# Layer 1 of a four-layer graph network in 64x64 tiles of the TensorE array, with one block of targets open at a time

## The chip, the cores and the metric

The kernel runs on one core of one Trainium2 chip. The metric is the device time of one execution in microseconds; a kernel's time is the median over its runs. A profile is one execution taken by the hardware profiler. In it PE is TensorE's matmuls and PEld its weight loads, DVE is VectorE, ACT is ScalarE, POOL is GpSimd, and SP is SyncE, which here issues the loads.

## What is computed

Four graph layers run one after the other over 4096 nodes with 64 features each. All use the same dense 4096 x 4096 matrix `adj` of float32 (64 MiB), and each has a layer norm and a relu in front and a residual behind. The change lies in layer 1, and touches the end of layer 0:

```python
# layer 0
h = relu(layernorm(x));  x = x + relu((adj @ h) @ W0.T + b0)
# layer 1
h = relu(layernorm(x))
h = lorentz_linear(h, W, b, scale)            # 64 -> 64, rows normed
q = lorentz_linear(h, Wq, bq, scale_q)
k = lorentz_linear(h, Wk, bk, scale_k)
att = 2.0 + 2.0 * (qm @ k.T)                  # qm: q with its first column negated
att = adj * sigmoid(att / att_scale + att_bias)
support = att @ h
x = x + support / sqrt(clip(abs(inner(support))))
```

Layer 2 needs all pairwise distances on a Poincare ball and the row sums of `adj` (the degrees); layer 3 needs, for each row, the rank of its nonzeros. Neither is edited.

## The kernel before

**Tiling.** `adj` comes transposed, sources on partitions, targets along the free dimension. A block `ib` is 512 targets (`W`), and there are 8 of them. A group `g` is 256 sources: a tile of 128 partitions x 2 x 512 (`G` = 2), one load of 512 KB, and there are 16 per block. Layer 1 works in pairs of groups, so 8 pairs per block and 64 in all. In this document A stands for the attention matmuls of one pair and S for its sums; the fifth A is that of the fifth pair.

**One pair of layer 1.** `l1_atts` puts q against k into PSUM (tile `mm`). The contraction is 64 long, so the two row halves of the array hold two chunks of 128 sources at once: tiles of 64 rows x 128 columns, 4 matmuls in the program for a pair, which the profile shows as 8 instructions, since one f32 matmul of 512 columns is two. `l1_sigmoids` reads PSUM on ScalarE and writes `sig`. `l1_weights` multiplies `sig` by `adj` on VectorE ("weighing"). `l1_sums`, through `pair_sum`, multiplies by h (`HL`), with a contraction of 128 and 64 output rows: the two column halves of the array hold two chunks at once, tiles of 128 rows x 64 columns. The lower half of the partitions of the accumulator `acc` holds the sum over the even chunks, the upper half that over the odd ones. `after1` evicts `acc` on ScalarE and adds the two halves with a matmul by `twice` (two identities on top of each other).

**Buffers.** PSUM has two `mm` tiles of two banks each, so one pair is in flight there. Up to six `sig` tiles are in use (`SIG`), and a sigmoid waits for the sum six groups back. There are two accumulator banks, taken by `ib % 2`, for layer 0 as for layer 1, so a new block's sums can begin while the old block is evicted. `adj` has ten load buffers in these two layers; a buffer is free when its last reader has run.

**Order.** Loads are issued on SP in the order of the list `order`: the last `EARLY` groups of layer 0 alternate with the first groups of layer 1. The list `l1` sets the order of layer 1's work: blocks 0 and 1 first take their groups 0 to 13 (`BEHIND` = 14), then both take groups 14 and 15, and from block 2 on every block is taken whole. Groups 14 and 15, a block's eighth pair, are sources 3584 to 4095, so they need h, q and k of block 7, whose row work is the last to come out of layer 0. That row work is `after0` and `before1`: eviction, projection by W0T, layer norm, transposition (h), projection by W1T, norms, transposition (HL), projection by WqkT, norms, transpositions (qq, k). Each step is handed from TensorE to ScalarE, VectorE or POOL, which takes square roots and powers. While it runs, `after1` and `before2` of other blocks may run as well, two at a time. Degrees are summed on VectorE (`dg`), some groups in layer 0 and some in layer 1.

A planner (`in_turn`) issues the whole program once, step by step, always the step that can start first by its own estimates; each engine then runs its instructions in exactly that order. So the order is fixed before the run, and an instruction that waits holds everything behind it on its engine.

Of the kernel before, what the change touches and what calls it, by code (L numbers as in the profile page):

```python
# [19 lines left out]
D = 64  # L20
# [3 lines left out]
NB = N // W  # L24
CB = W // P
G = 2
NG = NC // G
LEFT = (3, 7, 11, 15)
FRONT = (4,5,6,7,)
WAIT = 0.6  # L30
EARLY = 12
BEHIND = NG - CB // G
LATE = BEHIND - CB // G
HG = NG // 2
# [15 lines left out]
ON_V, ON_S = "DVE", "ACT"  # L50
# [94 lines left out]
def kernel(ctx: ExitStack, tc: tile.TileContext, a: dict, out: bass.AP):  # L145
# [4 lines left out]
    pace = Pace()  # L150
    PE, DVE, ACT, POOL = (
        InOrder(tc, e, pace, name)
        for e, name in (
            (nc.tensor, "PE"), (nc.vector, "DVE"), (nc.scalar, "ACT"), (nc.gpsimd, "POOL"),
        )
    )
# [144 lines left out]
    def cs(ib):  # L301
        return slice(ib * CB, (ib + 1) * CB)

    def ws(ib):
        return slice(ib * W, (ib + 1) * W)
# [4 lines left out]
    def rt(name, shape, dtype=F32):  # L310
        return rows.tile(shape, dtype, tag=f"{name}_{slot['now']}", name=name, bufs=1)
# [7 lines left out]
    def power(out, v, p):  # L319

        POOL.tensor_tensor(out, v, halves[p][:, 0 : v.shape[1], :], ALU.pow)
# [28 lines left out]
    def bank():  # L350
        k = spare.pop(0)
        t = (ps_two if k else ps_tr).tile([P, W], F32, tag=f"tr{k}", name="tr")
        in_use.append((t, k))
        return t
# [241 lines left out]

    def after1(ib, acc, st):
        e = rows.tile([P, W], F32, tag="e", name="e")
        ACT.copy(e, acc)
        st["acc_free"][ib % 2] = pace.latest  # L600
        yield ON_V, lambda: st["dg_done"].get((1, ib)) if (1, ib) in st["dg"] else 0.0
        dg = st["dg"].get((1, ib))
        if dg is not None:
            DVE.tensor_add(dg[:, 0, :], dg[:, 0, :], dg[:, 1, :])
        yield TURN
        ps = bank()
        v, n = ps[:, 0 : CB * D].rearrange("p (c k) -> p c k", k=D), CB * D
        for c in range(CB):
            b = slice(c * P, (c + 1) * P)
            PE.matmul(v[:, c, :], e[:, b], twice, start=True, stop=True)  # L610
            if dg is not None:
                PE.matmul(ps[:, n + c : n + c + 1], dg[:, 0, b], ones_f, start=True, stop=True)
        if dg is not None:
            st["dg_free"][ib % 2] = pace.latest
        yield ON_S
        s = rt("h", [P, CB, D])
        ACT.copy(s, v)
        sq = rt("r_sq", [P, CB, D])
        ACT.activation(sq, v, AF.Square)
        if dg is not None:  # L620
            new = rt("r_c", [P, CB, 1])
            ACT.copy(new, ps[:, n : n + CB].unsqueeze(2))
        yield ON_V
        if dg is not None:
            DVE.tensor_add(deg[:, cs(ib), :], deg[:, cs(ib), :], new)
        n = rt("r_n", [P, CB, 1])
        DVE.tensor_reduce(n, sq[:, :, 1:D], AX.X, ALU.add)
        DVE.tensor_sub(n, n, sq[:, :, 0:1])
        m = rt("r_m", [P, CB, 1])
        DVE.tensor_scalar(m, n, -1.0, None, ALU.mult)  # L630
        DVE.tensor_max(n, n, m)
        DVE.tensor_scalar(n, n, 1e-08, None, ALU.max)
        power(n, n, -0.5)
        yield ON_V
        DVE.tensor_mul(s, s, n.to_broadcast([P, CB, D]))
        DVE.tensor_add(x[:, cs(ib), :], x[:, cs(ib), :], s)
        yield ON_V
# [69 lines left out]
    def follow(gen, on=ON_V, evicts=False):  # L707

        tail.append(
            {"gen": gen, "on": on, "at": pace.latest, "slot": None, "evicts": evicts, "need": None}  # L710
        )
# [24 lines left out]
    def latest(*times):  # L736
        return None if None in times else max(times)
# [36 lines left out]
    def keep_warm(wait):  # L774
# [14 lines left out]
    st = {  # L789
        "h0": HA[:, :, 0:D],  # L790
        "dg": {}, "dg_done": {}, "acc_free": [0.0, 0.0], "dg_free": [0.0, 0.0],
    }
# [3 lines left out]
    def with_mark(layer, ib, *gens):  # L796
        for gen in gens:
            yield from gen
        rows_at[layer, ib] = pace.latest
# [30 lines left out]
    def take(k, d):  # L830

        return st["acc_free"][k] if d["first"] else 0.0
# [6 lines left out]
    def pair_tile(d):  # L839
        pair_tiles.append(d)  # L840
        turn = mm["count"] = mm["count"] + 1
        if mm["third"] is not None:
            d["ps"] = (ps_mm if turn % 3 else mm["third"]).tile([P, G, W], F32, tag="mm", name="mm")
        else:
            d["ps"] = ps_mm.tile([P, G, W], F32, tag="mm", name="mm")

    def pair_tiles_free():

        n = 2 if mm["third"] is None else 3
        a, b = (d.get("read") for d in pair_tiles[-n:][:2])  # L850
        return latest(a, None if b is None else b - 0.8)

    def acc_tile(k):
        return (ps_two if k else ps_acc).tile([P, W], F32, tag=f"acc{k}", name="acc")
# [17 lines left out]
    def group(layer, ib, g):  # L872
        degree = (g in (LEFT if ib else FRONT) and ib < NB - 1) == (layer == 1)
        return {"layer": layer, "ib": ib, "g": g, "degree": degree, "left": 1 + degree, "at": 0.0}
# [1 line left out]


    l0 = [group(0, ib, g) for ib in range(NB) for g in range(NG)]
    l1 = [group(1, ib, g) for ib in range(2) for g in range(BEHIND)]
    l1 += [group(1, ib, g) for ib in range(2) for g in range(BEHIND, NG)]  # L880
    l1 += [group(1, ib, g) for ib in range(2, NB) for g in range(NG)]
    order = l0[: len(l0) - EARLY] + [d for pair in zip(l0[len(l0) - EARLY :], l1) for d in pair]
    order += l1[EARLY:]
    done = {}
# [6 lines left out]
    accs = {}  # L891


    def pair_sum(d, by, t):
        k = d["layer"], d["ib"]
        if d["first"]:
            accs[k] = acc_tile(d["ib"] % 2)
            st["acc_free"][d["ib"] % 2] = None
        for c in range(G):
            PE.matmul(  # L900
                accs[k][c * D : (c + 1) * D, :], by[:, d["g"] * G + c, :], t[:, c, :],
                start=d["first"], stop=d["last"], skip_group_check=True,
            )
        return accs[k]

    def degree_sums(layer, work):
# [25 lines left out]
    def l0_sums():  # L932
        for d in l0:
            yield "PE", lambda: latest(
                arrival(d), rows_at.get((0, d["g"] * G // CB)), take(d["ib"] % 2, d),
                None if d["last"] and loads else 0.0,
            )
            acc = pair_sum(d, st["h0"], d["adj"])
            used(d)
            if d["last"]:  # L940
                ib = d["ib"]
                follow(with_mark(1, ib, after0(ib, acc, st), before1(ib, st)), ON_S, evicts=True)
# [17 lines left out]
    def l1_atts():  # L960
        for pair in pairs:
            yield "PE", lambda: latest(
                *(rows_at.get((1, d["g"] * G // CB)) for d in pair),
                rows_at.get((1, pair[0]["ib"])), pair_tiles_free(),
            )
            for d in pair:
                pair_tile(d)
                for c in range(G):
                    half = slice(c * D, (c + 1) * D)
                    PE.matmul(  # L970
                        d["ps"][:, c, :], st["kT"][half, d["g"], :],
                        st["qT"][half, ws(d["ib"])], start=True, stop=True,
                    )
                d["dist"] = pace.latest

    def l1_sigmoids():
# [15 lines left out]
    def l1_sums():  # L992
        for pair in pairs:
            yield "PE", lambda: latest(
                *(d.get("weighed") for d in pair), take(pair[0]["ib"] % 2, pair[0])
            )
            for d in pair:
                acc = pair_sum(d, st["HL"], d["att"])
                d["summed"] = pace.latest
            if d["last"]:  # L1000
                ib = d["ib"]
                follow(with_mark(2, ib, after1(ib, acc, st), before2(ib, st)), ON_S, evicts=True)
# [483 lines left out]
    def l3_sum():  # L1486
# [15 lines left out]
        if d["last"]:  # L1502
            follow(after3(ib, acc, st), ON_V, evicts=True)

    last = work[L3_AT:]
    order23 = work[:L3_AT] + [d for pair in zip(last, l3) for d in pair] + l3[len(last) :]
    in_turn([
        feed(order, "early"), feed(order23, "second"), second_tables(), second_part(), third_part(), third_tile(), l2_loads2(),
        l0_sums(), l1_sums(), l1_weights(), l1_sigmoids(), l1_atts(),
        in_steps(  # L1510
            (l2_dists(), -1, once), (l2_signs(), 0, once), (l2_sums2(), 2, if_two(1)),
# [58 lines left out]
```

## Time and profile before

Three runs took 1110.67 to 1120.76 us, median 1119.69. The profiled execution took 1116.49 us, of which its span is 1114.8.

| view | what | value |
|---|---|---|
| times | profiled execution / its span | 1116.49 / 1114.8 us |
| timeline | last layer 0 sum starts / last layer 1 sum ends | 207.2 / 482.8 us |
| groups | `mm<-qT,kT`, 512 instructions | 129.8 us busy, 624 ns each |
| groups | `acc<-sig,HL`, 512 instructions | 124.2 us busy, 605 ns each |
| groups | `sig<-mm` on ScalarE, 128 | 148.6 us busy, 1201 ns each |
| groups | `sig<-sig,adj` on VectorE, 128 | 152.6 us busy, 1221 ns each |
| groups | `e<-acc` copy on ScalarE, 128 x 512 | 586 ns each |
| groups | `e<-acc,others` add on VectorE, 65 x 512 | 682 ns each (layer 2) |
| DMA | `adj` loads | 512 x 512 KB, 5.5 us from issue to landing |

How to read it: a matmul instruction's length holds its way through the array, so two that follow each other overlap, and the time which a group takes is read from the start of one group to the start of the next. Successive operations on ScalarE and VectorE overlap by about 0.1 us for the same reason: sigmoids start 1.10 us apart and weighings 1.14. A shape such as `64*128` is the array's rows x columns that the instruction uses. The bracket at the end of a timeline row is the engine's idle time before it and what ended it.

### The profile page before, as it was taken

What the parts mean: (1) busy time and instruction counts of PE and PEld (TensorE: products, weight loads), DVE (VectorE), ACT (ScalarE), POOL (GpSimd) and SP (SyncE); (2) the same over time, 40 slices, a digit from 0 to 9 for tenths busy, and PEclk for the clock granted to TensorE, in tenths of its full rate; (3) what the DMA queues carried; (4) which work ended last, traced back from release to release, by engine and by line L of the source; (5) the groups of instructions that cost most, each with busy time, mean ns of one, the idle gap of its engine ahead of it and who ended that gap; (6) DMA issues with size and microseconds to landing.
All of it is one profiled execution on the core that took longest, in us unless ns stands there. A gap on an engine that the chain in (4) does not pass through costs nothing.

```text
span 1114.8 us, 15471 instructions
## 1 busy us (share of the span) xinstructions
PE 1053.7 (95%) x5300; PEld 471.2 (42%) x5300; DVE 917.6 (82%) x1496; ACT 795.5 (71%) x1279; POOL 259.9 (23%) x151
## 2 busy tenths in 40 slices
PE   6789999999999999999999999999999987999998
PEld 3234443334233333344454454544444443444444
DVE  7678989878998888758998999989989999766651
ACT  1045545686776777689988888879798776677776
POOL 3022222011111100043334334344443430000000
PEclk9899999999999999999999999999999999999999
DMA  8899999966677677544443444443435539999950
GB/s 305 314 365 409 407 383 363 325 229 225 218 235 244 235 255 248 177 164 163 159 170 141 181 172 144 176 170 138 183 120 217 177 129 353 378 409 409 411 238 10
DMA packets 77191, 271.76 MB, mean 244 GB/s; under 512 B 10040, under 2 KB 11064, under 8 KB 77112
## 3 DMA queue, kind: packets, MB, share of 16 engines
q1 hardware_dynamic: 75456, 270.57, 65.6%
q8 instruction: 42, 0.69, 0.2%
q10 hardware_dynamic: 1656, 0.20, 0.1%
q14 instruction: 37, 0.30, 0.1%
HBM read 269.68 MB, written 1.05 MB: 243 GB/s over the span
## 4 chain that ended last, share of the span: by engine, by line
PE 52%; DVE 19%; issue 8%; DMA 7%; ACT 7%; POOL 6%; SPq 0%; ACTq 0%; POOLq 0%; DVEq 0%
PE acc L137 26%; PE mm L137 16%; PE tr L137 11%; DMA adj<-in_adjT_dram 7%; POOL v L137 5%; DVE t L137 3%; DVE w L137 3%; DVE sig L137 3%; DVE dg L137 3%; ACT t L137 1%; ACT v L137 1%; ACT sig L137 1%; ACT lo_sq L137 1%; POOL lo_s L137 1%; DVE r_n L137 1%
## 5 line engine op out<-in xcount | busy, mean ns | idle before, releaser
L137 PE MATMUL acc<-w,HA 128*65 128x256 f32 (+1 forms) x736 | 247.9, 472 | 10.8 <-DVE w L137 10.7
L137 POOL TENSOR_SCALAR v<-v 128x1024 f32<-128x1024 f32 (+1 forms) x72 | 171.1, 2376 | 269.1 <-ACT v L137 269.1
L137 ACT ACTIVATE sig<-mm,att_b,att_a 128x1024 f32<-128x1024 f32 x128 | 148.6, 1201 | 50.8 <-PE mm L137 50.3
L137 DVE TENSOR_TENSOR sig<-sig,adj 128x1024 f32<-128x1024 f32 x128 | 152.6, 1221 | 29.9 <-ACT sig L137 28.0
L137 ACT ACTIVATE wt<-mm,down 128x1024 fp32r<-128x1024 f32 x128 | 136.1, 1111 | 44.3 <-PE mm L137 41.9
L137 DVE TENSOR_TENSOR dg<-dg,adj 128x1024 f32<-128x1024 f32 x113 | 137.7, 1221 | 7.6 <-DMA adj<-in_adjT_dram 6.0
L137 PE MATMUL acc<-adj,HA 128*64 128x512 f32 x512 | 125.7, 618 | 14.4 <-DMA adj<-in_adjT_dram 14.4
L137 PEld LDWEIGHTS acc<-w,HA 128*65 128x65 f32 x736 | 94.3, 138 | 95.1 <-issue 50.8
L137 PE MATMUL mm<-qT,kT 64*128 64x512 f32 x512 | 129.8, 624 | 2.8 <-ACT sig L137 2.0
L137 PE MATMUL acc<-sig,HL 128*64 128x512 f32 x512 | 124.2, 605 | 1.7 <-DVE sig L137 1.5
L137 ACT ACTIVATE v<-v,minus 128x1024 f32<-128x1024 f32 x72 | 79.1, 1098 | 30.1 <-POOL v L137 28.7
L137 DVE SCALAR_TENSOR_TENSOR t<-mm,t 128x1024 f32<-128x1024 f32 x72 | 83.5, 1160 | 19.7 <-PE mm L137 11.0
L137 DVE SCALAR_TENSOR_TENSOR t<-t,v 128x1024 f32<-128x1024 f32 x72 | 83.3, 1157 | 3.9 <-ACT t L137 3.4
L137 DVE TENSOR_TENSOR w<-t,adj 128x1024 f32<-128x1024 f32 x72 | 84.4, 1173 | 1.4
L137 DVE TENSOR_TENSOR w<-tr,adj 128x512 f32<-128x512 f32 x120 | 77.5, 683 | 8.5 <-PE tr L137 8.4
L137 ACT ACTIVATE t<-t 128x1024 f32<-128x1024 f32 x72 | 72.2, 1003 | 14.3 <-DVE t L137 14.2
L137 ACT ACTIVATE v<-mm 128x1024 f32<-128x1024 f32 x72 | 69.7, 967 | 15.8 <-PE mm L137 15.8
L137 PE MATMUL mm<-RT,LT 64*128 64x512 f32 (+1 forms) x288 | 79.0, 625 | 0.1
L137 PE MATMUL acc<-wt,S 128*128 128x512 f32 x256 | 75.6, 421 | 0.5 <-ACT wt L137 0.3
L137 ACT ACTIVATE t<-v 128x1024 f32<-128x1024 f32 x72 | 72.7, 1010 | 2.2
L137 PEld LDWEIGHTS mm<-qT,kT 64*128 64x128 f32 x512 | 43.8, 187 | 71.6 <-issue 34.5
L137 ACT ACTIVATE v<-v 128x1024 f32<-128x1024 f32 x72 | 72.1, 1001 | 0.0
(210 smaller groups left out, 1382.7 us busy)
## 6 DMA issues: line engine op xcount, KB each, us to landing
adj<-in_adjT_dram SPq DMA_DIRECT2D x512, 512.0 KB, 5.5
x<-in_x_dram SPq DMA_DIRECT2D x4, 256.0 KB, 3.6
out_dram<-h SPq DMA_DIRECT2D x8, 128.0 KB, 1.9
b<-in_b_dram ACTq DMA_DIRECT2D x2, 32.0 KB, 6.2
W<-in_W_dram ACTq DMA_DIRECT2D x3, 16.0 KB, 6.5
W0T<-in_W0T_dram ACTq DMA_DIRECT2D x2, 16.0 KB, 5.5
W1T<-in_W1T_dram ACTq DMA_DIRECT2D x1, 16.0 KB
W1T<-in_b_dram ACTq DMA_DIRECT2D x1, 0.2 KB
```

The costliest lines, as they stand in the source:

```text
L137: done = self.tc.keep_in_program_order(getattr(self.engine, op)(*args, **kw))
```

## The change

Layer 1's attention and sums both go to quarters of the array. For attention, each chunk's 128 sources are split into two halves `h`, so a pair has 8 matmuls of 64 rows x 64 columns in the program (16 instructions). For sums, `quarter_sum` splits the contraction: sources in the lower 64 partitions go to the first accumulator bank, those in the upper 64 to the second. A block thus takes both banks, and `after1` copies one on ScalarE and adds the other on VectorE. Since both banks are taken, no two blocks are open at a time: `l1` takes every block whole, the first two as well, and `EARLY` is 6 in place of 12. `pair_sum` stays, for layer 0 alone.

```diff
-EARLY = 12
+EARLY = 6
...
     def after1(ib, acc, st):
         e = rows.tile([P, W], F32, tag="e", name="e")
-        ACT.copy(e, acc)
-        st["acc_free"][ib % 2] = pace.latest
+        ACT.copy(e, acc[0])
+        st["acc_free"][0] = pace.latest
+        yield ON_V
+        DVE.tensor_add(e, e, acc[1])
+        st["acc_free"][1] = pace.latest
...
-    l1 = [group(1, ib, g) for ib in range(2) for g in range(BEHIND)]
-    l1 += [group(1, ib, g) for ib in range(2) for g in range(BEHIND, NG)]
-    l1 += [group(1, ib, g) for ib in range(2, NB) for g in range(NG)]
+    l1 = [group(1, ib, g) for ib in range(NB) for g in range(NG)]
...
+    def quarter_sum(d):
+        k = 1, d["ib"]
+        if d["first"]:
+            accs[k] = [acc_tile(r) for r in range(2)]
+            st["acc_free"][:] = [None, None]
+        for c in range(G):
+            for r in range(2):
+                source = slice(r * D, (r + 1) * D)
+                PE.matmul(
+                    accs[k][r][c * D : (c + 1) * D, :], st["HL"][source, d["g"] * G + c, :],
+                    d["att"][source, c, :], start=d["first"], stop=d["last"],
+                    skip_group_check=True,
+                )
+        return accs[k]
...
                 for c in range(G):
                     half = slice(c * D, (c + 1) * D)
-                    PE.matmul(
-                        d["ps"][:, c, :], st["kT"][half, d["g"], :],
-                        st["qT"][half, ws(d["ib"])], start=True, stop=True,
-                    )
+                    for h in range(2):
+                        to = slice(h * D, (h + 1) * D)
+                        PE.matmul(
+                            d["ps"][to, c, :], st["kT"][half, d["g"], to],
+                            st["qT"][half, ws(d["ib"])], start=True, stop=True,
+                        )
...
     def l1_sums():
         for pair in pairs:
             yield "PE", lambda: latest(
-                *(d.get("weighed") for d in pair), take(pair[0]["ib"] % 2, pair[0])
+                *(d.get("weighed") for d in pair), take(0, pair[0]), take(1, pair[0])
             )
             for d in pair:
-                acc = pair_sum(d, st["HL"], d["att"])
+                acc = quarter_sum(d)
                 d["summed"] = pace.latest
```

## The prediction

> **What bounds the kernel now.** I read the page first, for engine and slice, then the windows by stage, then the timeline of TensorE inside layer 1, then its timeline where layer 0 hands over to layer 1.
>
> ```profile
> span 1114.8 us, 15471 instructions
> ...
> PE 1053.7 (95%) x5300; PEld 471.2 (42%) x5300; DVE 917.6 (82%) x1496; ACT 795.5 (71%) x1279; POOL 259.9 (23%) x151
> ```
>
> The second view has two windows of the hand-over and two of layer 1's middle, each of the latter two target blocks long. Columns: length, busy time of each engine (instructions), granted clock, DMA share, GB/s.
>
> ```profile
> 175.70:208.30 32.60, 29.34 (x141) 10.72 (x140) 32.22 (x45) 21.63 (x72) 8.48 (x4) 1.00 0.94 348
> 208.30:268.00 59.70, 58.19 (x279) 22.91 (x280) 44.49 (x57) 42.27 (x76) 5.40 (x3) 1.00 0.75 256
> 307.30:376.90 69.60, 68.77 (x313) 25.00 (x313) 60.80 (x121) 49.02 (x87) 5.72 (x4) 1.00 0.71 243
> 376.90:446.40 69.50, 68.68 (x312) 24.89 (x312) 59.34 (x119) 48.93 (x87) 5.72 (x4) 1.00 0.71 242
> ```
>
> Layer 1 is bound by TensorE: 68.8 of 69.6 us, with VectorE at 87% and ScalarE at 70%. Before 208.3 it is DMA and VectorE that are full (0.94; 32.2 of 32.6 us). The third view is TensorE's timeline (start, length, instructions):
>
> ```profile
> 233.50 3.65 PE L137 MATMUL acc<-sig,HL 128*64 128x512 f32 x16
> 237.09 1.99 PE L137 MATMUL mm<-qT,kT 64*128 64x512 f32 x8
> ...
> 320.68 1.99 PE L137 MATMUL mm<-qT,kT 64*128 64x512 f32 x8
> 322.60 1.94 PE L137 MATMUL acc<-sig,HL 128*64 128x512 f32 x8
> 324.47 1.99 PE L137 MATMUL mm<-qT,kT 64*128 64x512 f32 x8
> 326.39 1.94 PE L137 MATMUL acc<-sig,HL 128*64 128x512 f32 x8
> 328.25 0.66 PE L137 MATMUL tr<-ident,r 128*128 128x128 f32 x4
> ```
>
> I call the mm group of a pair A and its acc group S. From start to start A takes 1.92 us and S 1.86 or 1.87. Two S in a row, with no change of array shape between them, take 3.59 (233.50 to 237.09), so the bare group is 1.72, and a change of shape costs 0.20 after A, 0.15 after S. The fourth view is the same timeline along block 7's row work, the chain from the last layer 0 sum to the k columns which each layer 1 block's eighth pair needs:
>
> ```profile
> 220.55 0.43 PE L137 MATMUL tr<-W0T,e 128*128 128x64 f32 x2
> ...
> 229.99 0.63 PE L137 MATMUL tr<-ident,h 128*64 128x128 f32 x4
> ...
> 239.17 0.60 PE L137 MATMUL tr<-ident,HL 128*64 128x128 f32 x4
> ...
> 241.68 1.16 PE L137 MATMUL tr<-WqkT,columns 65*128 65x128 f32 x8
> ...
> 253.19 0.66 PE L137 MATMUL tr<-ident,qq 128*128 128x128 f32 x4
> ...
> 254.80 1.99 PE L137 MATMUL mm<-qT,kT 64*128 64x512 f32 x8 [0.73 <-ACT kT L137]
> ```
>
> That chain is 34.2 us long, and TensorE was idle for 1.4 us of it: seven A and seven S of blocks 0 and 1 ran beneath it.
>
> **Part 1, the 64x64 shape.** Each A and each S becomes 16 instructions in place of 8, with half the array each. If four run at once, a group stays at 1.72 us. No row here shows four f32 quarters together. The nearest are four column strips in bf16 and the weight loads of the column halves:
>
> ```profile
> 952.31 0.40 PE L137 MATMUL tr<-RT,pick 128*32 128x512 bf16 x4
> ```
>
> ```profile
> 256.71 0.20 PEld L137 LDWEIGHTS acc<-sig,HL 128*64 128x64 f32 x4 [0.76 <-issue]
> ```
>
> Four matmuls end within 0.40 us where one has 0.38 in its group's row, and four weight loads of 0.14 us take 0.20 together, so neither stream is serial. The other bound is two at a time, 3.43 us a group; I take 1.72. The doubled weight loads (1,024 more at 0.14 us) then lie beneath steps of 0.43 us; were they serial, four would need 0.55 and add 0.12 to each of 512 steps, 61 us. The Trainium skill's page "TensorE: Matmul & The Clock Gate", Part 3, "The mechanism", speaks against the change here: weight loads overlap running matmuls only where the row groups differ, and two quarters of one row half share theirs. By it half the 16 loads of a group, 8 x 0.14 us, would be exposed, some 140 us over 128 groups (an estimate). Today's S has both column halves on the same rows, and its loads overlap all the same (0.20 us for four, S at 1.87 us), so the row decides.
>
> What is gained is the changes of shape. In the built order of the old program an A or S is followed by another shape 121 times (73 times by each other); in the new one 38 times. 83 x 0.178 us = **-14.7 us** (12.4 to 16.6 by the two prices).
>
> **Part 2, the start of layer 1.** Six early layer 1 loads fewer stand before layer 0's last load on SP's queue. At 1.28 us (410 GB/s, slices of layer 0) to 1.51 us (348 GB/s) each, the last layer 0 sum comes 8 us sooner, near 200. But a layer 1 sum now needs both banks, and bank 1 holds layer 0's block 7. So the first three S, which ran before 208.3, come after that block's eviction. In the new ScalarE order this stands behind block 6's q and k norms (copy to last square, 243.12 to 247.93: 4.8 us), then 0.59 itself: 205.6. Three S, 5.2 us, end at 210.8; the old program had done them at 208.3: **+2.5 us**. If the eviction were not held, -2.5; if block 7's degree sums on VectorE (full here) hold layer 0's tiles so that the last load gains nothing, +8.
>
> **Part 3, one block open.** Block 0's eighth pair needs block 7's k, and block 1 can't stand in. In the new order the chain's first projection (W0T) follows the fifth A, at 212.7. Its steps, with the durations of its last run: to h 10.4 us (sigmoids and weighings of two pairs in front of it on ScalarE and VectorE; was 9.4), to HL 9.9 (was 9.2), to qq 11.4 (0.6 transpose, 0.6 copy, 1.2 projection, 4.8 norms, 0.65 on VectorE, 2.5 root on POOL, 0.8 of copies, the rest handing over; was 14.0, with four sigmoids and weighings in front), to the eighth A 1.7: 33.4 us. Early blocks took 35 to 36; 31 is the shortest sum I can make. Beneath it stand only the sixth and seventh A and the fourth to seventh S (10.7 us) and the transposes and projections with their changes of shape (8 us). TensorE idles 4.3 before HL, 9.0 before qq and 1.4 around them: 14.7 us in place of 1.4, **+13.3 us** (10 to 16). Behind it on TensorE wait the eighth and ninth A, for them the sigmoids; the loads fill their ten buffers and stop.
>
> **Part 4, seven block boundaries.** A block's first S now waits for ScalarE's copy of bank 0 (0.59) and VectorE's add of bank 1 (new; 0.68 by the e<-acc,others row, 8 x 0.68 = 5.4 us in all). In the new order the copy stands behind six small copies, the add behind two weighings (1.14 us apiece), a degree copy and a degree add (0.62 and 1.14). Laid out from the last S of a block at 0: TensorE has an A and four transposes to do, until 4.3; the weighings end at 2.0, the degree work at 3.8, the add at 4.5. So this wait is 0.2 us. Then the order runs S, the eviction's matmuls, S and three A, the second and third of which go at ScalarE's pace (two sigmoids, 2.21 us, against 1.72): 1 us more, and 0.3 before the second S. 1.5 us x 7 = 10.5. The old blocks idle too: 69.55/2 = 34.8 us a block against 34.15 of groups and transposes, 0.63 x 7 = 4.4. Net **+6.1 us** (-4.4 for no wait; +19 at 3.4 each, if degree adds wait for their tiles and hold the add). The end of layer 1 has the added hop once: **+0.7**. Layers 2 and 3 keep their instructions and only shift.
>
> Sum: -14.7 + 2.5 + 13.3 + 6.1 + 0.7 = **+7.9 us**. The profiled execution took 1116.49 us (1114.8 span, 1.7 around it), so 1124.4; it lay 3.2 under the median of the three runs, 1119.69, from which it would be 1127.6. I say 1126.
>
> **Rivals.** *The shape pays* (0.17): block 7's chain finds cover, because without sigmoids and weighings queued in front it shrinks, and the eviction isn't held: part 3 at +3, part 2 at -2.5. Against it: the steps alone sum to 31 us, with 19 of other work to lay beneath. Price: -14.7 - 2.5 + 3 + 6.1 + 0.7 = -7.4, with boundaries at zero net -13.5; 1103 to 1112. It decides where TensorE idles under 5 us in the chain. *The boundaries are dear* (0.22): VectorE is at 87% already, and the add comes after degree adds that may wait for their tiles' loads; from 2 us of wait at each it decides, and at 3.4 us each, 7.9 + 13 = +21, 1137 to 1141. For it: nothing runs ahead after the second S. *The quarters don't run four at once* (0.05), the change not doing what it says: 128 x 1.72 = 220 us, about 1340; the bf16 strips speak against it. The forecast keeps 0.56.
>
> **Numbers.** About 1% is what a measurement of this kernel tells from no change, 11 us. The forecast's spread (parts 2 and 3 by 5 us each, boundaries by 8) puts 0.16 of its 0.56 above +1%, 0.02 below -1% and 0.38 within. The first rival gives 0.10 faster, 0.07 within; the other two are slower. Faster 0.12, same 0.45, slower 0.43. The range reaches into both near rivals: 1110 to 1143, leaving out 0.05 above for the quarters and about 0.07 at either end.
>
> **What would show it.** In the changed profile: 16 instructions of A or S in 1.7 to 1.8 us, with no step between neighbours; TensorE idle for 4 us before HL, 9 us before qq of block 7, near 228 to 245, released by VectorE and ScalarE; the last layer 0 sum near 200 and the first S after 205; boundaries a period of 33 to 34 us. It is wrong if a group takes over 1.9 us, if TensorE's busy share stays whole at the hand-over, or if TensorE waits over 3 us for the add at each boundary.

## The result, and the profile after

The changed kernel took 1134.12 us, median of four runs (1133.29 to 1139.1), beside 1116.38 for the kernel before: 1.016 times as long, 95% interval 1.0122 to 1.0198. A second series of six runs gave 1132.40 beside 1117.68, ratio 1.0145 (1.0115 to 1.0175); the ratios here and below are the recorded estimates and differ slightly from the quotient of the two medians. So the change costs 15 to 18 us; 8 had been forecast. The profiled execution is the 1139.1 us one. It lies above the other three, and its first sigmoid of layer 1 starts 4.5 us later than the old kernel's (91.0 against 86.5 us), after equal work. In the profile of the second series (1130.74 us) that start is 84.9, and what follows, up to the start of layer 2, lies within 0.3 us of the first profile when counted from it. Times below are therefore counted from the first sigmoid where kernels are compared. Of the eight runs of e7 below, one took 2345.27 us, the others 1123.93 to 1131.66, and it is left out there.

The page of the changed kernel, engines and granted clock by slice of 28.4 us:

```profile
span 1137.4 us, 17578 instructions
...
PE 1058.6 (93%) x6328; PEld 478.0 (42%) x6346; DVE 922.4 (81%) x1504; ACT 794.7 (70%) x1279; POOL 263.6 (23%) x151
...
PEclk9879999869999999999999999999999999999999
```

The instructions have grown by 2,107, TensorE's busy time by only 5 us: no sign of quarters that run one after the other. The clock row has a dip in the third slice, which belongs to the late start of this run, and a new one in the eighth and ninth, 199 to 256 us, which is the hand-over from layer 0. The windows say more. Four of them cover the hand-over, two the middle of layer 1 (columns: length, busy time of PE, PEld, DVE, ACT, POOL, granted clock, DMA share, GB/s):

```profile
189.43:203.45 14.02, 14.02 (x95) 5.30 (x91) 13.46 (x20) 9.12 (x22) 4.41 (x2) 1.00 0.87 302
204.46:216.25 11.79, 8.33 (x51) 2.45 (x53) 10.21 (x13) 6.63 (x24) 2.15 (x1) 0.71 0.89 313
218.48:237.43 18.95, 15.61 (x134) 7.03 (x132) 12.93 (x21) 10.76 (x24) 2.92 (x2) 1.00 0.70 231
237.43:257.64 20.21, 9.52 (x51) 4.62 (x54) 5.04 (x9) 9.81 (x30) 2.49 (x1) 0.58 0.01 2
334.70:404.60 69.90, 67.35 (x569) 24.51 (x568) 61.73 (x122) 48.67 (x86) 7.38 (x4) 1.00 0.72 242
404.60:474.50 69.90, 67.92 (x585) 24.95 (x589) 60.81 (x124) 49.61 (x90) 7.39 (x4) 1.00 0.72 243
```

In the last hand-over window TensorE is busy for 9.5 of 20.2 us, nothing is loaded (0.01), and what runs has a clock of 0.58. In the middle two blocks take 69.9 us where they took 69.5 to 69.6: faster groups, yet no shorter blocks. TensorE's timeline shows the groups in a stretch without a wait:

```profile
344.96 1.90 PE L137 MATMUL mm<-qT,kT 64*64 64x512 f32 x16
346.68 1.90 PE L137 MATMUL acc<-sig,HL 64*64 64x512 f32 x16
348.39 1.90 PE L137 MATMUL mm<-qT,kT 64*64 64x512 f32 x16
350.11 1.90 PE L137 MATMUL acc<-sig,HL 64*64 64x512 f32 x16
```

From start to start it is 1.72 us for A and for S: the bare group, with no price for a change of shape. The hand-over on the same timeline, where the bracket gives the idle time ahead and what ended it:

```profile
203.45 1.08 PE L137 MATMUL acc<-adj,HA 128*64 128x512 f32 x4
204.46 1.07 PE L137 MATMUL acc<-sig,HL 64*64 64x512 f32 x2
208.99 7.42 PE L137 MATMUL acc<-sig,HL 64*64 64x512 f32 x43 [3.46 <-ACT e L137]
...
218.48 0.43 PE L137 MATMUL tr<-W0T,e 128*128 128x64 f32 x2
...
237.43 0.60 PE L137 MATMUL tr<-ident,HL 128*64 128x128 f32 x4 [3.35 <-DVE HL L137]
238.69 2.07 PE L137 MATMUL tr<-WqkT,columns 65*128 65x128 f32 x8 [0.67 <-ACT columns L137]
249.93 1.12 PE L137 MATMUL tr<-ident,qq 128*128 128x128 f32 x4 [9.17 <-ACT qq L137]
250.84 0.63 PE L137 MATMUL tr<-ident,k 128*128 128x128 f32 x2
252.00 4.40 PE L137 MATMUL mm<-qT,kT 64*64 64x512 f32 x24 [0.52 <-ACT kT L137]
```

Two instructions of the first S start behind layer 0's last sum and the rest waits 3.5 us for bank 1. Then the chain of block 7 takes 33.5 us (218.48 to 252.00), with 3.35, 0.67, 9.17 and 0.52 us idle. The last row has 24 instructions in 4.40 us, where 16 take 1.72: the first 16 of them need 3.31 us (to 255.31), about half speed, the last eight run at full speed. The granted clock is half from 207.19 to 214.01 and from 237.91 to 254.97 us. A block boundary, first on TensorE, then on VectorE:

```profile
364.10 1.07 PE L137 MATMUL acc<-sig,HL 64*64 64x512 f32 x2
365.74 1.94 PE L137 MATMUL acc<-sig,HL 64*64 64x512 f32 x14 [0.56 <-DVE e L137]
...
373.79 2.18 PE L137 MATMUL mm<-qT,kT 64*64 64x512 f32 x16 [0.47 <-ACT sig L137]
376.20 2.18 PE L137 MATMUL mm<-qT,kT 64*64 64x512 f32 x16 [0.23 <-ACT sig L137]
```

```profile
359.73 1.22 DVE L137 TENSOR_TENSOR dg<-dg,adj 128x1024 f32<-128x1024 f32 x1
360.87 2.35 DVE L137 TENSOR_TENSOR sig<-sig,adj 128x1024 f32<-128x1024 f32 x2
363.14 0.69 DVE L137 COPY dg<-adj 128x1024 f32<-128x1024 f32 x1
363.86 1.23 DVE L137 TENSOR_TENSOR dg<-dg,adj 128x1024 f32<-128x1024 f32 x1
365.00 0.68 DVE L137 TENSOR_TENSOR e<-e,acc 128x512 f32<-128x512 f32 x1
```

S takes from 364.10 to 367.61 until the next operation, 1.63 us more than a group without a wait: its first two instructions find bank 0 free, and the other bank is free only when the add ends, at 365.68. VectorE has not been idle for more than 0.1 us since 348.70; the add stands behind 1.9 us of degree work. With the three A behind it at ScalarE's pace (0.65 us ahead of the second, 0.97 over the second and third), a boundary stalls TensorE for 3.25 us. From ScalarE's copy (to 362.73) the add is 2.27 us late. It is so at five of the seven boundaries; at the first and the last it follows the copy by 0.1 and 0.4 us.

To compare kernels I count the sums done (64 in all), and give in us the time from the first sigmoid until the n-th was done, for the kernel before, and what the others need more. The last row is the start of layer 2's sixteenth `v`.

| sums done | before | changed | e1: order alone | e9: block 0 full width | e10: three remedies | e2: mixed |
|---|---|---|---|---|---|---|
| 7 | 139.8 | +3.3 | +6.5 | +6.6 | +4.9 | +0.2 |
| 8 | 143.6 | +24.9 | +20.2 | +20.4 | +17.2 | +0.2 |
| 16 | 181.6 | +19.3 | +17.8 | +14.9 | +11.7 | +0.2 |
| 24 | 220.1 | +15.8 | +14.2 | +11.4 | +6.3 | -0.2 |
| 56 | 359.2 | +16.5 | +15.8 | +12.2 | +3.1 | -3.8 |
| 64 | 396.3 | +12.7 | +14.4 | +8.4 | -3.5 | -5.1 |
| layer 2 | 482.9 | +17.1 | +14.4 | +12.2 | +2.5 | -4.4 |

The column of the changed kernel tells the story: a loss between the seventh and the eighth sum, part of it won back by the 24th, no gain over the next four blocks, a gain in the last, and 4.4 us lost where layer 2 begins.

### The profile page after: what moved, and what is told of

Read it like the earlier page. It is cut to its first block, busy times and chain, and to the rows that moved or that the text cites. A ratio compares the mean times of both kernels' runs of the same rounds, so it can differ in the third digit from the quotient of the medians.

```text
span 1137.4 us, 17578 instructions
## 1 busy us (share of the span) xinstructions
PE 1058.6 (93%) x6328; PEld 478.0 (42%) x6346; DVE 922.4 (81%) x1504; ACT 794.7 (70%) x1279; POOL 263.6 (23%) x151
## 4 chain that ended last, share of the span: by engine, by line
PE 50%; DVE 22%; issue 9%; ACT 7%; POOL 6%; DMA 6%; SPq 0%; ACTq 0%; DVEq 0%; POOLq 0%
PE acc L137 25%; PE mm L137 13%; PE tr L137 12%; DVE sig L137 6%; DMA adj<-in_adjT_dram 5%; POOL v L137 4%; DVE w L137 3%; DVE t L137 3%; DVE dg L137 2%; ACT lo_sq L137 1%; ACT t L137 1%; POOL lo_s L137 1%; POOL r_n L137 1%; DVE r_n L137 1%; DVE e L137 1%
## 5 line engine op out<-in xcount | busy, mean ns | idle before, releaser
L137 PE MATMUL acc<-adj,HA 128*64 128x512 f32 x512 | 127.8, 628 | 11.7 <-DMA adj<-in_adjT_dram 11.3
L137 PE MATMUL acc<-sig,HL 64*64 64x512 f32 x1024 | 130.7, 607 | 7.0 <-ACT e L137 3.5
L137 PE MATMUL mm<-qT,kT 64*64 64x512 f32 x1024 | 127.7, 602 | 5.1 <-ACT sig L137 4.5
L137 ACT ACTIVATE v<-mm 128x1024 f32<-128x1024 f32 x72 | 69.6, 966 | 16.0 <-PE mm L137 15.9
L137 PEld LDWEIGHTS mm<-qT,kT 64*64 64x64 f32 x1024 | 36.3, 134 | 85.1 <-issue 49.3
```

Source lines behind the costliest of these rows:

```text
L137: done = self.tc.keep_in_program_order(getattr(self.engine, op)(*args, **kw))
```

## The experiments

Theory: the hand-over (parts 2 and 3) is most of the loss, and the boundaries, through the add, eat what the shape gains. Rivals: the boundaries alone; a wait for ScalarE's copy in place of the add.

**e1: the order alone.** Full-width matmuls and one bank a block.

```diff
-EARLY = 12
+EARLY = 6
...
-    l1 = [group(1, ib, g) for ib in range(2) for g in range(BEHIND)]
-    l1 += [group(1, ib, g) for ib in range(2) for g in range(BEHIND, NG)]
-    l1 += [group(1, ib, g) for ib in range(2, NB) for g in range(NG)]
+    l1 = [group(1, ib, g) for ib in range(NB) for g in range(NG)]
```

> The kernel before with the order of the changed kernel alone: six early loads, layer 1 block by block, full-width matmuls, one accumulator bank a block. Theory (the loss sits at the hand-over from layer 0 to layer 1, where the chain of layer 1's preparation no longer has two blocks' groups to cover it): 11 to 16 us longer than the kernel before, 1127 to 1133 us beside 1116, with TensorE idle 13 to 19 us between the last sum of layer 0 and the eighth attention group, and block ends in layer 1 as cheap as before (some 0.6 us each). Rival (two banks and the waits at block ends are the loss, the order costs little): 0 to 4 us longer. If the order alone costs more than the whole change (over 18 us), the quarters gain more than the block ends lose.

Measured: 1131.06 against 1117.92, 13.1 us longer, ratio 1.0117 (1.0079 to 1.0156). TensorE's timeline:

```profile
203.15 1.89 PE L137 MATMUL acc<-sig,HL 128*64 128x512 f32 x8
...
207.79 0.43 PE L137 MATMUL tr<-W0T,e 128*128 128x64 f32 x2 [0.83 <-ACT e L137]
...
244.84 1.11 PE L137 MATMUL tr<-ident,qq 128*128 128x128 f32 x4 [7.30 <-ACT qq L137]
```

The idle times of the hand-over come to 12 us (0.83, 1.79, 1.37, 7.30 and 0.52 the larger ones), under the expected 13 to 19, and the table shows nothing lost after it. So the order alone explains most of the change's loss, at the place where theory had it. Not all of it is idle time: the granted clock is half from 210.13 to 216.96 and from 240.85 to 251.09 us, and TensorE is busy for 6.83 and 5.73 us of these. Half of that, some 6 of the 13 us, is an estimate of what the slower clock can cost. With one bank the first S also run among layer 0's last sums, and the chain's projection by W0T comes 5.5 us behind the last layer 0 sum instead of 15.0.

**e2: mixed.** Blocks 0 and 1 as in the kernel before, quarters from block 2 on.

```diff
-EARLY = 6
+EARLY = 12
...
-        ACT.copy(e, acc[0])
+        if ib < 2:
+            ACT.copy(e, acc)
+            st["acc_free"][ib % 2] = pace.latest
+        else:
+            ACT.copy(e, acc[0])
...
-                acc = quarter_sum(d)
+                acc = pair_sum(d, st["HL"], d["att"]) if d["ib"] < 2 else quarter_sum(d)
```

The attention matmuls take the same condition, and the list `l1` is the old one.

> Blocks 0 and 1 of layer 1 as before (both open at a time, full-width matmuls, twelve early loads), quarters and two banks for blocks 2 to 7 alone. Theory (hand-over is most of the loss; quarters gain about 0.17 us a switch of mode, 6 blocks x some 10 = 11 us, and block ends with a wait for the VectorE add take 3.25 us each, 6 x 2.6 more than before = 16): 0 to 5 us longer than the kernel before, that is 13 to 18 us shorter than the changed kernel. Rival (the waits at block ends are most of the loss): some 10 to 13 us longer than before, 5 to 8 shorter than the changed kernel.

Measured: 1109.72 against 1117.92, ratio 0.9942 (0.9917 to 0.9968): 8 us shorter than the kernel before, more than either theory had. The hand-over's loss is gone to within 0.2 us (table), and six blocks of quarters gain 5 us by the traces. So this version beats both kernels, and my price for its boundaries, 16 us, was too high: they are not the changed kernel's. In this order the add follows the copy by 0.03 to 0.7 us in all six of these blocks, so that the S of a new block hardly waits. VectorE's timeline at one of them (the copy ends at 343.39):

```profile
341.49 2.36 DVE L137 TENSOR_TENSOR sig<-sig,adj 128x1024 f32<-128x1024 f32 x2 [0.79 <-ACT sig L137]
343.77 0.68 DVE L137 TENSOR_TENSOR e<-e,acc 128x512 f32<-128x512 f32 x1
344.37 1.22 DVE L137 TENSOR_TENSOR dg<-dg,adj 128x1024 f32<-128x1024 f32 x1
```

The degree sum comes behind the add here, without any rule for it: the planner's order with the old start of layer 1 has it so.

**e3: the add first.** The degree sums of layer 1 stay back on VectorE while a block is handed over.

```diff
         DVE.tensor_add(e, e, acc[1])
         st["acc_free"][1] = pace.latest
+        st["open"] = False
...
-                arrival(d, 4.0), st["dg_free"][d["ib"] % 2] if first else 0.0
+                arrival(d, 4.0), st["dg_free"][d["ib"] % 2] if first else 0.0,
+                None if st.get("open") else 0.0,
...
             if d["last"]:
                 ib = d["ib"]
+                st["open"] = True
```

> The changed kernel, with layer 1's degree sums held back on VectorE from a block's last sum until the add of the second bank, so that the add follows the copy at once. Theory (the next block's first sum waits 1.63 us a block end for the add, which stands behind 1.9 us of degree sums): 8 to 11 us shorter than the changed kernel; the 14 matmuls start within 0.4 us of the first two; block period 33.4 to 33.9 us instead of 34.95. Rival (the wait is for ScalarE's copy of the first bank, and the add is late only with it): 0 to 2 us shorter. Third way: the degree sums held back delay the next groups' weighing, and the wait only moves there, 0 to 4 us shorter with a new idle ahead of the sums behind it.

Measured: 1127.16, ratio 1.0095 (1.0058 to 1.0131) to the kernel before, 5 us under the changed kernel's 1132.40 (7 under 1134.12). The same place on TensorE and on VectorE:

```profile
355.32 2.15 PE L137 MATMUL acc<-sig,HL 64*64 64x512 f32 x16
357.40 0.43 PE L137 MATMUL tr<-twice,e 128*128 128x64 f32 x2
```

```profile
352.51 2.36 DVE L137 TENSOR_TENSOR sig<-sig,adj 128x1024 f32<-128x1024 f32 x2 [0.79 <-ACT sig L137]
354.79 0.68 DVE L137 TENSOR_TENSOR e<-e,acc 128x512 f32<-128x512 f32 x1
355.38 1.22 DVE L137 TENSOR_TENSOR dg<-dg,adj 128x1024 f32<-128x1024 f32 x1
```

The add follows the weighing, and the S takes 2.15 us with all 16 instructions in one piece instead of 3.57 in two. That shows the wait was for the add, and the add was behind degree work. At the last sum the kernel is 7.4 us ahead of the changed one (+5.3 against +12.7 to the kernel before); 1.6 of that is given back where layer 2 begins. The degree sums held back behind the last block are not the reason: e5 and e10 do not hold these back and lose as much as e3 between the last sum and layer 2 (6.0 us, the changed kernel 4.4). What the reason is stays open. The size was below the expected 8 to 11, which took all boundaries for alike; 1.63 us at the five late ones are 8.2.

**e4: no add.**

```diff
-        st["acc_free"][0] = pace.latest
-        yield ON_V
-        DVE.tensor_add(e, e, acc[1])
-        st["acc_free"][1] = pace.latest
+        st["acc_free"][0] = st["acc_free"][1] = pace.latest
```

> The changed kernel without the add of the second bank: the sources of the upper half are left out of layer 1's sums as they are passed on, so the output is not the reference's; all matmuls remain. The second bank is free when the copy of the first is. Theory: as with the add put first, 9 to 12 us shorter than the changed kernel; the block period falls from 34.95 to some 33.5 us, with what is left of the idle at block ends (1.6 us each) paced by ScalarE. Rival (the copy is what the sum waits for): 0 to 2 us shorter.

Measured: 1123.85, ratio 1.0042 (1.0017 to 1.0067), 8.5 us under the changed kernel: just short of theory's 9 to 12, far from the rival's 0 to 2. Its gain holds through layer 2's start (+7.2 at the last sum, +7.1 there), while the changed kernel goes from +12.7 to +17.1. So the add is also part of what the end of layer 1 costs; e3 says that its place on VectorE, not its 0.68 us, is most of the price.

**e5: mixed, and the add first.** e2 with e3's edit for blocks 2 to 6.

> Blocks 0 and 1 as before, quarters for blocks 2 to 7, and the degree sums held back on VectorE while a block is handed over (not behind the last block). Theory (the two costs found so far, the hand-over and the wait for the add, are separate and can be taken away together): 2 to 6 us shorter than the mixed kernel without it (1109.7), so 1104 to 1108, 9 to 14 us shorter than the kernel before. Rival (in the mixed kernel the sums stand later behind the block ends and hardly wait for the add; what is idle there is ahead of attention groups, 6.1 of 8.4 us): no difference to the mixed kernel within 2 us.

Measured: 1112.16, ratio 0.9949 (0.9923 to 0.9975), against 0.9942 for e2 alone. The rival was right that nothing is gained in all: in the mixed kernel the add is on time, and the wait for it is not there to be taken away. By the table's count the edit puts the last sum 3.3 us sooner (-8.4 against -5.1), and layer 2 begins 2.0 us later (-2.4 against -4.4). The same edit is worth 5 to 7 us in one order and nothing in another.

**e6: twelve early loads** in the changed kernel.

```diff
-EARLY = 6
+EARLY = 12
```

> The changed kernel with twelve early loads instead of six. Theory (the first three sums wait for the eviction of the last block of layer 0, not for loads): within 2 us of the changed kernel. Rival (with six, the adjacency of block 0's later groups comes late or layer 0's loads move): 3 to 6 us shorter. With twelve the buffers may also be taken from layer 0's own transfers, then up to 5 us longer.

Measured: 1142.01, ratio 1.0197 (1.0157 to 1.0238), 9.6 us longer than the changed kernel: none of the three expectations. TensorE's timeline says why:

```profile
195.59 1.98 PE L137 MATMUL acc<-adj,HA 128*64 128x512 f32 x4 [2.32 <-DMA adj<-in_adjT_dram]
...
206.60 1.08 PE L137 MATMUL acc<-adj,HA 128*64 128x512 f32 x4 [1.34 <-DMA adj<-in_adjT_dram]
212.56 1.12 PE L137 MATMUL tr<-ident,qq 128*128 128x128 f32 x4 [4.89 <-ACT qq L137]
213.61 1.98 PE L137 MATMUL acc<-adj,HA 128*64 128x512 f32 x4
```

Layer 0's last sums wait for loads which the six additional early ones have pushed back: the last one starts 12.0 us later after the first sigmoid than with six (213.61 - 89.2 against 203.45 - 91.0). Its load is issued 8.2 us later (203.52 - 89.2 against 197.08 - 91.0); the rest is the transposition of qq ahead of it, which waits 4.89 us for ScalarE. In the changed kernel that delays the one thing that matters, the chain. So the smaller `EARLY` is not a part of the loss; without it the change would have cost 23 us (1142.01 against 1118.58).

**e7: idle matmuls at the hand-over.** The kernel keeps a routine that issues matmuls into a spare tile while TensorE waits; it was closed during layer 1.

```diff
-        if wait < WAIT or not spare or l1[0].get("dist") and "tables" not in opened or "third" in opened:
+        hand_over = "summed" in l0[-1] and "dist" not in l1[BEHIND]
+        if wait < WAIT or not spare or l1[0].get("dist") and "tables" not in opened and not hand_over or "third" in opened:
...
             acc = pair_sum(d, st["h0"], d["adj"])
+            d["summed"] = pace.latest
             used(d)
```

> The changed kernel with idle matmuls of the kind it issues elsewhere (on a tile of their own, results not read) allowed while TensorE waits at the hand-over. Theory (TensorE's granted clock falls to half at 207.2 to 214.0 and 237.9 to 255.0 us because it was idle for 3.5 and 9.2 us, and groups there take twice as long): the clock stays at 1.0 there, and the kernel is 3 to 5 us shorter than the changed one, 1129 to 1131. Rival (the clock's fall costs nothing, since the chain through VectorE and ScalarE ends as late): 0 to 1 us. If the idle matmuls delay the chain's own short groups, it gets longer.

Measured: 1127.49, ratio 1.0089 (1.0058 to 1.0121), 4.9 us under the changed kernel. The windows of the same stretch as above, then the idle matmuls behind the projection by WqkT and the eighth A:

```profile
206.62:228.56 21.94, 19.88 (x154) 8.47 (x151) 16.82 (x28) 11.47 (x24) 4.17 (x3) 0.92 0.73 250
228.56:247.32 18.76, 14.85 (x122) 9.94 (x126) 6.14 (x10) 9.69 (x30) 1.64 (x1) 1.00 0.18 57
```

```profile
232.19 5.52 PE L137 MATMUL tr<-ident 128*128 128x128 f32 x48
...
242.90 1.95 PE L137 MATMUL mm<-qT,kT 64*64 64x512 f32 x16 [0.24 <-ACT kT L137]
245.32 2.19 PE L137 MATMUL mm<-qT,kT 64*64 64x512 f32 x16 [0.47 <-ACT sig L137]
```

The clock is 1.00 in the last stretch where it was 0.58, and the A runs at full speed. By the table's count it is 4.4 us ahead at the sixteenth sum (+14.9) and at the last (+8.3). The test is not quite clean: the planner also moved one S and an A behind the chain's first step. Of the 4.4 us the changed kernel's rows show about 3.5 as speed: 46 sums in 7.3 us which at 0.1075 us each take 4.9, and 5.64 us from the eighth A to the S behind the ninth, which e7 does in 4.42. Some 1.4 more lie within the chain, in the projection by WqkT (2.07 against 1.16) and the transposition of qq (1.12 against 0.66); e7's chain is longer for the work moved into it. The clock records give a second estimate: at half clock TensorE is busy for 5.02 and 6.70 us in the changed kernel and for 3.42 us in e7 (211.86 to 215.28), and half of the difference is some 4 us. How much of the gain comes from the moved work is not separated.

**e8: attention at full width.**

```diff
-                    for h in range(2):
-                        to = slice(h * D, (h + 1) * D)
-                        PE.matmul(
-                            d["ps"][to, c, :], st["kT"][half, d["g"], to],
-                            st["qT"][half, ws(d["ib"])], start=True, stop=True,
-                        )
+                    PE.matmul(
+                        d["ps"][:, c, :], st["kT"][half, d["g"], :],
+                        st["qT"][half, ws(d["ib"])], start=True, stop=True,
+                    )
```

> The changed kernel with the attention groups at full width again (64x128 tiles, 8 matmuls a pair), the sums in quarters and two banks. Theory (a switch between attention and sums costs 0.18 us as long as their tiles differ, and nothing when both are 64x64; some 83 switches are the changed kernel's gain): 11 to 15 us longer than the changed kernel, 1145 to 1149, with 3.8 us from one attention group to the next in an undisturbed stretch instead of 3.43. Rival (quarters gain by running four at once in the sums alone): 0 to 4 us longer.

Measured: 1144.15, ratio 1.0233 (1.02 to 1.0267), 11.7 us longer than the changed kernel.

```profile
307.01 1.99 PE L137 MATMUL mm<-qT,kT 64*128 64x512 f32 x8
308.93 1.95 PE L137 MATMUL acc<-sig,HL 64*64 64x512 f32 x16
310.81 1.99 PE L137 MATMUL mm<-qT,kT 64*128 64x512 f32 x8
```

From A to A it is 3.80 us, in the changed kernel 3.43 (344.96 to 348.39). The sums in quarters alone gain nothing; it is the common shape that gains 0.37 us a pair.

**e9: block 0 at full width**, in one bank, quarters from block 1 on, order as in the changed kernel.

```diff
-                *(d.get("weighed") for d in pair), take(0, pair[0]), take(1, pair[0])
+                *(d.get("weighed") for d in pair), take(0, pair[0]), take(1, pair[0]) if pair[0]["ib"] else 0.0
...
-                acc = quarter_sum(d)
+                acc = quarter_sum(d) if d["ib"] else pair_sum(d, st["HL"], d["att"])
```

> The changed kernel with block 0 of layer 1 at full width in one bank, quarters and two banks from block 1 on; the order stays block by block. Theory (5 us of the hand-over come from the second bank: the first sums cannot start among layer 0's last ones and stand 3.5 us before the eviction of block 7, which moves the whole chain; in the run with the order alone, TensorE idled 12 us there against 17 in the changed kernel): 3 to 6 us shorter than the changed kernel, with the first sums of layer 1 among the last of layer 0. Rival (the chain of the preparation is as long either way, and the second bank only moves the idle time about): 0 to 1 us shorter, or up to 2 longer, as block 0 loses its 3 us of quarters.

Measured: 1127.62, ratio 1.0112 (1.0075 to 1.0149), 4.8 us under the changed kernel of the same series. The intervals of the two overlap; the traces, which agree between the two profiles of the changed kernel in this count, say 4.5 us at the eighth sum and 4.9 in layer 2.

```profile
192.37 1.08 PE L137 MATMUL acc<-adj,HA 128*64 128x512 f32 x4
193.28 1.89 PE L137 MATMUL acc<-sig,HL 128*64 128x512 f32 x8
...
197.75 0.43 PE L137 MATMUL tr<-W0T,e 128*128 128x64 f32 x2 [0.66 <-ACT e L137]
```

No S waits for a bank between layer 0's last sum and the projection, which comes 5.4 us behind it, as in e1.

**e10: the three together**: e9, e3's edit for all blocks but the first and the last, e7's idle matmuls.

> Block by block as in the changed kernel, with the three remedies together: block 0 at full width in one bank, the degree sums held back while a block but the last is handed over, idle matmuls at the hand-over. Theory (second bank at the hand-over 3 to 6 us, wait for the add 7 to 9, clock 4 to 6, separate from one another, though the clock's share shrinks with the idle time): 13 to 18 us shorter than the changed kernel, 1116 to 1121, about level with the kernel before; what is left of the order's 13 us is the chain itself. Rival (they overlap, each takes the same idle time): 7 to 10 us shorter, no better than the best one of them by more than 3 us.

Measured: 1117.70, ratio 0.9992 (0.9964 to 1.0021): level with the kernel before, 14.7 us under the changed kernel. The single gains (4.8, 5.2 and 4.9) add to 14.9, and by the table's count at the last sum 4.3, 7.4 and 4.4 add to 16.1 where the three together gain 16.2. So the three costs are separate ones in the main. At the sixteenth sum they overlap a little: e9 and e7 are 4.4 us ahead each, the three together 7.6.

**e11: the changed kernel again.**

> The changed kernel itself beside the two runs of this call, as the base for differences of a few us: 1130 to 1137 us. If its profiled run is again near the top of its runs, the half-clock stretch at 64 to 77 us that the first profile showed belongs to the kernel's start and not to chance.

Measured: 1132.40 (1130.57 to 1136.8), the base used above. Its profile has no late start (first sigmoid at 84.9 us), so that the start of the first profile is a matter of the run.

## Why the forecast was right in direction and 7 to 10 us short

The sign and the main mechanisms held: the shape's gain and the idle time of the chain were sized well. One term was missing, and the wait for the add and the end of layer 1 were sized too small; a part of these errors was made up by chance, since blocks without a stall were shorter than I had them. What was missing shows when the prediction's terms are set along the table, with a block's share of the shape at -1.84 (14.7 / 8) and a boundary at +0.87 (6.1 / 7):

| stretch | forecast, us | measured, us |
|---|---|---|
| to 24 sums: parts 2 and 3, three blocks, two boundaries | 15.8 - 5.5 + 1.7 = +12.0 | +15.8 |
| 24 to 56 sums: four blocks and boundaries | -7.4 + 3.5 = -3.9 | +0.7 |
| 56 to 64 sums | -1.8 + 0.9 = -0.9 | -3.8 |
| end of layer 1 | +0.7 | +4.4 |
| sum | +7.9 | +17.1 |

**Part 1 held.** Four quarters run at once (1.72 us a group), and the doubled weight loads lie beneath. The rule that I weighed against the rows, in the Trainium skill's page "TensorE: Matmul & The Clock Gate", Part 3, "The mechanism", that loads overlap only where row groups differ, would have put some 140 us on the kernel; the measured group leaves no room for it. Giving the attention its old shape back cost 11.7 us (e8), against 14.7 in the prediction for the whole change of shape. That fits the price I had: by the traces an A or S is followed by another shape 106 times in e8 and 38 times in the changed kernel, and 68 x 0.178 us is 12.1 us.

**Part 2 held in its events.** Counted with the old kernel's start, the last layer 0 sum came at 199 (said: 200) and the first S went on at 204.5 (said: 205.6), held by the eviction of block 7. That the six loads fewer bring the sums forward is shown by e6, where the last load is issued 8.2 us later (said: 8). The three S then took 7.3 us, not 5.2, because of the clock. The +2.5 us was the net of sooner loads and the wait for the second bank, a net that no run measures by itself. Singly, e6 gives 9.6 us for the loads and e9 4.8 us at least for the bank, since e9 gives up block 0's quarters too.

**Part 3 held in its events:** the chain took 33.5 us (said: 33.4), with idle times of 3.35 before HL and 9.17 before qq (said: 4.3 and 9.0). e1 shows that the order, its six loads fewer included, costs 13.1 us. That this is close to the +13.3 of this part is partly luck, since some 6 us of it can be the slower clock, which I had at nothing, while the loads work the other way. The eighth A's wait does not end the loss, however: the groups behind it ran at half speed up to 255 us. **A term was missing**, the price of TensorE's clock behind an idle stretch; e7 took back 4.9 us, about 3.5 of them seen as speed. All windows that I had quoted of the kernel before have a granted clock of 1.00, and I carried the full speed over into a stretch that I myself had said would be idle for 15 us. The same page of the Trainium skill, Part 1, "What's actually happening", says that the clock goes to half after an idle window of about 3.4 us and comes back after a busy one; the idle 3.46 and 9.17 us here, in windows with a clock of 0.71 and 0.58, agree, and from that page the term could have been put in. As a bound its figure does not hold here: in e1 and e9 the clock fell to half behind idle times of 1.79 and 2.46 us (at 210.13 and 201.79 us; 0.83 and 0.66 us idle shortly ahead of these), while the kernel before kept 1.00 over an idle 2.23 us ahead of 207.23.

**Part 4 was mis-sized: the wait for the add.** I had 0.2 us of 1.5; it was 1.63 of 3.25. From the start of a block's last S (359.92) TensorE is done with its other work at 4.2 us, as I had said (4.3). But the weighings end at 3.3, not at 2.0, the degree work at 5.2, not at 3.8, and the add at 5.8, not at 4.5: another degree sum, at 359.73, stands ahead of the weighings, and I had begun counting VectorE's queue behind it. What else the boundary costs, at ScalarE's pace, was 1.62 (said: 1.3). e3 and e4 show by how much the add matters: 5 to 9 us. The rival that called the boundaries dear, at 3.4 us, had the size of the stall right, not its reason (no row of degree work at the boundary waits for a load), and its total, 1137 to 1141, too high, since a block without its stalls takes 34.95 - 3.25 = 31.7 us, under the 32.3 that I had (34.15 - 1.84), and since two of the boundaries have the add on time, the last among them, which agrees with the gain in the last eight sums. Of the signs that I had listed, the period of a block is the one that missed: 34.95 us, not 33 to 34.

**The end was mis-sized,** +4.4 in place of +0.7. Layer 2's first transpositions wait for VectorE and ScalarE with the last block's eviction:

```profile
501.42 1.11 PE L137 MATMUL tr<-twice,e 128*128 128x64 f32 x8 [0.72 <-DVE e L137]
502.36 0.61 PE L137 MATMUL tr<-ident,rb 128*128 128x128 f32 x4
503.64 3.35 PE L137 MATMUL tr<-ident 128*128 128x128 f32 x16 [0.67 <-ACT RB L137]
```

With the row work of the block before the last (`rb`, `lb`) still to be done there, the added hop is only a part. Without the add that loss is gone (e4), in e1 and e2 it hardly appears, and with the add put first it is 6.0 us (e3, e5 and e10); which of its steps the order moves, and why the planner moved them, was not tried.

The rival in which the shape pays by a chain with cover fell: the chain idles for 13.7 us. It pays where the chain is left its cover, in e2.

## What to carry to other kernels

A gain in a busy engine's instructions is worth what the order leaves of it: here the same quarters lose 15 us with one block open and gain 8 when the first two blocks stay open in pairs, so take the new shape where its resource (the second bank) is not the cover of a chain. Price an added wait by the whole queue that stands ahead of it on its engine, from the last moment at which that engine was idle. And where an edit makes TensorE idle for a few us, add the slower clock around and behind the idle stretch to the idle time itself; here 1.79 us behind 0.83 us were enough for it in e1, and 2.23 us in the kernel before were not.

## What the runs showed of the hardware

Four f32 quarters of 64x64 run at once, 16 instructions in 1.72 us, with a weight load beneath each of them. Quarters in the sums alone gain nothing over full-width strips (S from start to start 1.88 us between A of another shape). The granted clock was half from 207.19 to 214.01 us, around an idle time of 3.46 us, and from 237.91 to 254.97 us, behind 3.35 and around 9.17 us, and was still low in the 5 us behind the longer one. In e1 and e9 it fell behind 1.79 and 2.46 us (0.83 and 0.66 us shortly ahead). With short idle matmuls in place of a part of the waiting, and some work moved, the kernel was 4.9 us shorter.
